# Inverse roots on VectorE for four tiles at once, and layernorm and gate as a queue of small jobs, in a sparse attention and expert kernel

## The chip, the cores and the metric

The kernel runs on one core of a Trainium2 chip. A core has five engines that run their own instruction streams in order and wait for one another by semaphores: TensorE (PE in the profile, its weight loads as PEld), VectorE (DVE), ScalarE (ACT), GpSimd (POOL) and SyncE (SP). The metric is the device time of one execution in microseconds, as the median of several runs.

## The reference

The input is a graph of 4096 nodes with 512 features and a 0/1 adjacency. The layer is an attention over neighbours with 8 heads of 64, then a mixture of 8 experts of which each node takes the best 2. Both read a layernorm and are added to their input.

```python
def _layernorm(x, axis=-1, eps=1e-5):
    m = jnp.mean(x, axis=axis, keepdims=True)
    v = jnp.var(x, axis=axis, keepdims=True)
    return (x - m) / jnp.sqrt(v + eps)

# attention
adj = jnp.maximum(adjacency_matrix, eye)
q, k, v = (jnp.einsum('nd,hdk->hnk', node_matrix, W) for W in (Wqs, Wks, Wvs))
scores = jnp.einsum('hqk,hmk->hqm', q, k) * kd ** (-0.5)
scores = scores + IDENTITY_BIAS * eye - MASK_VAL * (1.0 - adj)
att = jax.nn.softmax(scores, axis=-1)
return jnp.einsum('hqm,hmk,hko->qo', att, v, Wo)

# experts
logits = xf @ Wg + bg
topk_scores, topk_idx = jax.lax.top_k(logits, 2)
topk_w = jax.nn.softmax(topk_scores, axis=-1)
h = jax.nn.gelu(jnp.einsum('nd,edh->neh', xf, W1) + b1, approximate=False)
y = jnp.einsum('neh,ehf->nef', h, W2) + b2
# the sum of topk_w * y over the two chosen experts

x = x + attention(_layernorm(x), adj, ...)
x = x + experts(_layernorm(x), ...)
```

## The kernel before

The kernel goes through three stages. The projection stage takes 32 tiles of 128 nodes through layernorm and the projections to q, k and v, which go to DRAM, and beside this makes for each tile a list of the nodes that are a neighbour of any of its 128 queries. The attention stage goes through 395 items: for each tile its own 128 keys and then, 363 in all, chunks of 128 keys of its list. GpSimd gathers the rows of k and v and of the adjacency of each chunk by indirect DMA, 7 items ahead. The expert stage runs 71 tiles of sorted nodes through the two matrices of their expert.

The layernorm's mean and variance are taken on VectorE; the inverse root (a first guess from the bits of the number and three Newton steps) on GpSimd, for one tile at a time, one number per partition:

```python
def mean_var(pool, xin, name):
    stats = pool.tile([P, nc.vector.BN_STATS_DIM], F32, tag="stats", name=f"stats_{name}")
    nc.vector.bn_stats(stats, xin)
    mv = pool.tile([P, nc.vector.BN_AGGR_DIM + 2], F32, tag="mv", bufs=6, name=f"mv_{name}")
    nc.vector.bn_aggr(mv[:, :2], stats)
    nc.gpsimd.tensor_scalar(mv[:, 1:2], mv[:, 1:2], EPS, None, op0=ALU.add)      # L155
    nc.gpsimd.tensor_scalar(                                                     # L157
        mv[:, 2:3].bitcast(I32), mv[:, 1:2].bitcast(I32), -0.5, float(0x5F3759DF),
        op0=ALU.mult, op1=ALU.add,
    )
    m, v, r, t = (mv[:, j : j + 1] for j in range(4))
    for _ in range(3):
        nc.gpsimd.tensor_scalar(t, r, r, v, op0=ALU.mult, op1=ALU.mult)          # L163
        nc.gpsimd.tensor_scalar(t, t, -0.5, 1.5, op0=ALU.mult, op1=ALU.add)      # L164
        nc.gpsimd.tensor_mul(r, r, t)                                            # L165
    nc.gpsimd.tensor_scalar(t, m, r, -1.0, op0=ALU.mult, op1=ALU.mult)           # L166
    return mv

def normalize(pool, dst, xin, mv, name):
    nc.scalar.activation(dst, xin, AF.Identity, bias=mv[:, 3:4], scale=mv[:, 2:3])   # L171
```

One step of the attention stage fetches an item far ahead, transposes the keys of item n+3, takes the scores of n+2, the values of n, and then does what is due of the tiles that have ended (`later`). `masked` is the product of the exponentials with the mask, and `values` ends with the running sum of the exponentials, both on VectorE.

```python
for n, (i, c) in enumerate(items):
    if n + AHEAD < len(items):
        fetch(n + AHEAD)          # L687: two indirect DMAs by GpSimd; one scatter (L565) if any waits
    # ...
    if n + 3 < len(items):
        turn(n + 3)               # PE L703, ACT L706
    if n + 2 < len(items):
        scores(n + 2)             # PE L719, ACT L729
    values(n)                     # PE L748, DVE L754
    later(n)
    if n + 2 < len(items):
        masked(n + 2)             # DVE L736
    if c == listed[i] - 1:
        left.append((n, i))
```

`later(n)` calls `piece(i, n - n0)` for the tiles that have ended: each piece k is due k steps after the end of its tile. The `e` buffers are two banks of PSUM.

```python
def piece(i, k):
    # ...
    if k == 1:      # sums of the exponentials over the keys, for 8 heads in 4 x 32 rows and 2 halves
        sums[i] = ps_e.tile([P, 2, P], F32, tag="e", name=f"sums_{i}")
        a = acc.pop(i).rearrange("k (r j u) q -> k r u j q", r=2, u=2)
        for r in range(4):
            nc.tensor.matmul(
                sums[i][r * Q4 : (r + 1) * Q4], ones32, a[:, r % 2, r // 2],
                start=True, stop=True, tile_position=(0, r * Q4),
            )
    if k == 2:
        rinv[i] = single.tile([P, 2, P], F32, tag="rinv", name=f"rinv_{i}")
        nc.vector.reciprocal(rinv[i], sums[i])                                   # L776
        # ... a test of the sums on ACT (L778)
        load_x(i)
    if k == 3:      # the reciprocals spread over the rows of each head
        # ... 2 matmuls of 256 columns (L783), and a test of rinv on ACT
    if k == 4:
        o = osb[i]
        nc.vector.tensor_mul(o, o, rb.pop(i).rearrange("p j u q -> p (j u) q"))
    if k == 5:
        # ... 4 matmuls with Wo (L795)
    if k == 6:
        xt = x_in[i]
        nc.vector.tensor_add(xt, xt, py.pop(i))
        nc.sync.dma_start(out=out[ts(i, P), :], in_=xt)
        mv[i] = mean_var(small, xt, f"b{i}")
    if k == 7:
        # ... rows of a group of tiles, once per group
        normalize(small, row[g][:, j, :D], x_in.pop(i), mv.pop(i), f"b{i}")
    if k == 8:
        x2T[i] = gate_1(i, row[g][:, j, :D], single, ps_e, "e")    # 4 transposes (PE L177), copy (ACT L178)
    if k == 9:
        l4[i] = gate_2(i, x2T.pop(i), single, ps_e, "e")           # gate product (PE), copy (ACT)
    if k == 10:
        gate_3(i, l4.pop(i), lg[g][:, j], ps_e, "e")               # logits (PE), bias (DVE)
    if j < m - 1:
        return
    # k == 11 to 14, once per group of m tiles: ranks, places, weights, then scatters of the rows
```

Groups have 4 tiles, and the last three have 2, 1 and 1. Ranks count the nodes that went to each expert before:

```python
    for j in range(m):
        nc.vector.tensor_copy(counts[:, j], count)
        nc.vector.tensor_add(count, count, chosen[:, j])
```

In the projection stage the same layernorm runs a block of 4 tiles ahead, one tile in a step, with the load of x two steps before its statistics.

Of the kernel before, what the change touches and what calls it, by code (L numbers as in the profile page):

```python
# [32 lines left out]
def kernel(  # L33
# [115 lines left out]
    def mean_var(pool, xin, name):  # L149

        stats = pool.tile([P, nc.vector.BN_STATS_DIM], F32, tag="stats", name=f"stats_{name}")
        nc.vector.bn_stats(stats, xin)
        mv = pool.tile([P, nc.vector.BN_AGGR_DIM + 2], F32, tag="mv", bufs=6, name=f"mv_{name}")
        nc.vector.bn_aggr(mv[:, :2], stats)
        nc.gpsimd.tensor_scalar(mv[:, 1:2], mv[:, 1:2], EPS, None, op0=ALU.add)  # L155

        nc.gpsimd.tensor_scalar(  # L157
            mv[:, 2:3].bitcast(I32), mv[:, 1:2].bitcast(I32), -0.5, float(0x5F3759DF),
            op0=ALU.mult, op1=ALU.add,
        )  # L160
        m, v, r, t = (mv[:, j : j + 1] for j in range(4))
        for _ in range(3):
            nc.gpsimd.tensor_scalar(t, r, r, v, op0=ALU.mult, op1=ALU.mult)  # L163
            nc.gpsimd.tensor_scalar(t, t, -0.5, 1.5, op0=ALU.mult, op1=ALU.add)  # L164
            nc.gpsimd.tensor_mul(r, r, t)  # L165
        nc.gpsimd.tensor_scalar(t, m, r, -1.0, op0=ALU.mult, op1=ALU.mult)  # L166
        return mv

    def normalize(pool, dst, xin, mv, name):

        nc.scalar.activation(dst, xin, AF.Identity, bias=mv[:, 3:4], scale=mv[:, 2:3])  # L171
# [14 lines left out]
    with tc.tile_pool(name="adjT", bufs=3) as ap, tc.tile_pool(  # L186
# [181 lines left out]
        def tokens_1(i):  # L368
            mvs[i] = mean_var(work, xts[i], f"a{i}")

        def tokens_2(i):
            xns[i] = work.tile([P, D], F32, tag="xn", name=f"xn_{i}")
            normalize(work, xns[i], xts.pop(i), mvs.pop(i), f"a{i}")
# [67 lines left out]
        for t in range(TPB):  # L441
            tokens_2(t)
            tokens_3(t)
        list_constants()


        load_at = {7 * i // 4: i for i in range(NT)}
        lists_from = {7 * (g * G + G - 1) // 4 + 3: g for g in range(NTB)}
        for u in range(8 * NTB + 1):
            b, s = divmod(u, 8)  # L450
            if u in load_at:
                load_adj(load_at[u])
            due = []
            for k in range(8):
                if u - k in lists_from:
                    due += lists_at(lists_from[u - k], k)
            nxt = (b + 1) * TPB
            if b < NTB:
                if b + 1 < NTB:
                    if s < 4:  # L460
                        load_x(nxt + s)
                    if 2 <= s < 6:
                        tokens_1(nxt + s - 2)
                    if 3 <= s < 7:
                        tokens_2(nxt + s - 3)
                if s < 4:
                    project_kv(b, s)
                else:
                    if s == 4:
                        qT = block.tile([P, NP, TB], F32, tag="qT", name=f"qT_{b}")  # L470
                    project_q(b, s - 4, qT)
                    if s == 7:
                        nc.sync.dma_start(out=qT_d[:, :, ts(b, TB)], in_=qT)
                if b + 1 < NTB and s >= 4:
                    tokens_3(nxt + s - 4)
            if u - 2 in load_at:
                neighbours(load_at[u - 2])
            for f in due:
                f()


    def gate_1(i, row, pool, psum, tag):

        xT = pool.tile([P, DC, P], F32, tag="x2T", name=f"x2T_{i}")
        transposed(psum, xT, row, f"b{i}", tag)
        return xT

    def gate_2(i, xT, pool, psum, tag):
        pg = psum.tile([P, P], F32, tag=tag, name=f"pg_{i}")
        for c in range(DC):  # L490
            nc.tensor.matmul(
                pg[c * Q4 : (c + 1) * Q4], wg[:, c, :], xT[:, c, :], start=True, stop=True,
                tile_position=(0, c * Q4),
            )
        l4 = pool.tile([P, P], F32, tag="l4", name=f"l4_{i}")
        nc.scalar.copy(l4, pg)
        return l4

    def gate_3(i, l4, l, psum, tag):
        pl = psum.tile([P, E], F32, tag=tag, name=f"pl_{i}")  # L500
        nc.tensor.matmul(pl, l4, gather4, start=True, stop=True)
        nc.vector.tensor_add(l, pl, bg_sb)

    def route_1(m, l, pool, name):
# [15 lines left out]
        for j in range(m):  # L520
            nc.vector.tensor_copy(counts[:, j], count)
            nc.vector.tensor_add(count, count, chosen[:, j])
        return rank, chosen, counts

    def route_2(m, chosen, counts, psum, tag, name):

        pp = psum.tile([P, m, E], F32, tag=tag, name=f"pp_{name}")
        nc.tensor.matmul(pp, below, chosen, start=True, stop=False)
        nc.tensor.matmul(pp, ones, counts, start=False, stop=True)
# [108 lines left out]
    with tc.tile_pool(name="kv", bufs=AHEAD + 1) as kvp, tc.tile_pool(  # L638
# [14 lines left out]
        spread = single.tile([P, 2, P], F32, name="spread")  # L653
        nc.vector.memset(spread, 0.0)
        for u in range(2):
            for r in range(2):
                q = (2 * u + r) * Q4
                nc.vector.memset(spread[q : q + 1, u, r * KD : (r + 1) * KD], 1.0)
# [100 lines left out]
        DONE = "e"  # L759

        def piece(i, k):
# [3 lines left out]
            if k == 1:  # L765

                sums[i] = ps_e.tile([P, 2, P], F32, tag="e", name=f"sums_{i}")
                a = acc.pop(i).rearrange("k (r j u) q -> k r u j q", r=2, u=2)
                for r in range(4):
                    nc.tensor.matmul(  # L770
                        sums[i][r * Q4 : (r + 1) * Q4], ones32, a[:, r % 2, r // 2],
                        start=True, stop=True, tile_position=(0, r * Q4),
                    )
            if k == 2:
                rinv[i] = single.tile([P, 2, P], F32, tag="rinv", name=f"rinv_{i}")
                nc.vector.reciprocal(rinv[i], sums[i])  # L776
                test = single.tile([P, 2, P], F32, tag="test", name=f"test_{i}")
                nc.scalar.activation(test, sums.pop(i), AF.Copy, accum_out=fine[:, i, 0:1])  # L778
                load_x(i)
            if k == 3:  # L780
                rb[i] = ps_e.tile([P, 2, 2, P], F32, tag="e", name=f"rb_{i}")
                for u in range(2):
                    nc.tensor.matmul(  # L783
                        rb[i][:, :, u, :], spread[:, u], rinv[i], start=True, stop=True
                    )
                test = single.tile([P, 2, P], F32, tag="test", name=f"test2_{i}")
                nc.scalar.activation(test, rinv.pop(i), AF.Copy, accum_out=fine[:, i, 1:2])
            if k == 4:
                o = osb[i]
                nc.vector.tensor_mul(o, o, rb.pop(i).rearrange("p j u q -> p (j u) q"))  # L790
# [7 lines left out]
            if k == 6:  # L798
                xt = x_in[i]
                nc.vector.tensor_add(xt, xt, py.pop(i))  # L800
                nc.sync.dma_start(out=out[ts(i, P), :], in_=xt)
                mv[i] = mean_var(small, xt, f"b{i}")
            if k == 7:
                if j == 0:
                    row[g] = small.tile([P, m, W], F32, tag="rows", name=f"rows_{g}")
                    lg[g] = small.tile([P, m, E], F32, tag="l", name=f"l_{g}")
                    nc.vector.tensor_copy(
                        row[g][:, :, D].bitcast(I32), ids[:, i0 : i0 + m]
                    )
                normalize(small, row[g][:, j, :D], x_in.pop(i), mv.pop(i), f"b{i}")  # L810
            if k == 8:
                x2T[i] = gate_1(i, row[g][:, j, :D], single, ps_e, "e")
            if k == 9:
                l4[i] = gate_2(i, x2T.pop(i), single, ps_e, "e")
            if k == 10:
                gate_3(i, l4.pop(i), lg[g][:, j], ps_e, "e")
            if j < m - 1:
                return
            if k == 11:
                ranks[g] = route_1(m, lg[g], small, f"{g}")  # L820
            if k == 12:
                rank, chosen, counts = ranks[g]
                ranks[g] = rank, route_2(m, chosen, counts, ps_e, "e", f"{g}")
            if k == 13:
                rank, pp = ranks.pop(g)
                slots_i[g] = route_3(m, lg.pop(g), rank, pp, row[g], small, f"{g}")
            if k == 14:
                for t in range(m):
                    for s in range(2):
                        waiting.append(lambda t=t, s=s: route_4(row[g], slots_i[g], t, s))  # L830

        LAST = 14
        left = []

        def later(n):
            for n0, i in left:
                piece(i, n - n0)

# [9 lines left out]
        for n, (i, c) in enumerate(items):  # L848
            if n + AHEAD < len(items):
                fetch(n + AHEAD)  # L850
# [21 lines left out]
        for n in range(len(items), len(items) + LAST + 1):  # L872
            later(n)
            while waiting:
                waiting.pop(0)()

# [26 lines left out]
    with tc.If(again > 0):  # L903
# [81 lines left out]
        with tc.tile_pool(name="g3", bufs=1) as one, tc.tile_pool(  # L985
# [4 lines left out]
            with tc.For_i(0, N, P) as t0:  # L990
# [5 lines left out]
                m = mean_var(one, xt, "g")  # L996
                normalize(one, rows[:, 0, :D], xt, m, "g")
                xT = gate_1("g", rows[:, 0, :D], one, psum, "a")
                lg4 = gate_2("g", xT, one, psum, "b")
                l = one.tile([P, 1, E], F32, name="gl")  # L1000
                gate_3("g", lg4, l[:, 0], psum, "c")
# [146 lines left out]
```

## Time and profile before

| | |
|---|---|
| median of 3 runs | 2644.12 us (2635.33 to 2649.11) |
| the profiled execution | 2492.47 us, span 2490.7 us |
| PE, PEld busy | 2175.0 us (87%), 1449.5 us (58%) |
| DVE, ACT, POOL busy | 1522.2 us (61%), 968.8 us (39%), 1467.1 us (59%) |
| first gather, last gather | 413 us, 1838 us |
| first matmul of the expert stage | 1926 us |

Busy time is the time in which an engine executes; issuing, waiting and semaphores are not in it. A share of the whole span mixes three stages with different limits, so windows of time and the waits of each stage tell more. In the answers, `out<-in` names the tiles that an instruction writes and reads, and L with a number is a line of the kernel. The profiled execution is shorter than the timed runs; stage lengths below are those of the profiled one.

### The profile page before, as it was taken

How to read it: one execution, taken by the hardware profiler on the slowest of the kernel's cores; microseconds unless marked ns; L12 is line 12 of the kernel's file. 1: busy time of each engine (PE TensorE's matmuls, PEld its weight loads, DVE VectorE, ACT ScalarE, POOL GpSimd, SP SyncE). 2: the span in 40 equal slices, each digit the busy share in tenths (PEclk: the TensorE clock that was granted, in tenths of full speed). 3: DMA queues.
4: the chain of work that ended last, by engine and by line, in shares of the span. 5: the costliest groups of instructions: out<-in, count | busy, mean ns of one | idle time of the engine just before them, and what ended most of it. 6: DMA issues, size and time to landing. Idle time of an engine off the chain costs nothing. (4 is left out here: it accounts for less than half of the span.)

```text
span 2490.7 us, 50730 instructions
## 1 busy us (share of the span) xinstructions
PE 2175.0 (87%) x19898; PEld 1449.5 (58%) x19898; DVE 1522.2 (61%) x2101; ACT 968.8 (39%) x1834; POOL 1467.1 (59%) x1711
## 2 busy tenths in 40 slices
PE   6899997888888997988988888878872999999998
PEld 3344444777776775776766767666651444444444
DVE  3787782877777786777777777767662233333332
ACT  2222221555554553555554545545430222222222
POOL 4665564877877787787888878778751122112111
PEclk9999998989988998998999999989885999999999
DMA  6758873666667676666666566556536656656654
GB/s 266 275 203 309 306 279 139 184 193 212 197 209 222 211 217 213 197 218 195 202 181 200 182 188 211 185 178 188 184 121 218 135 136 137 133 137 139 136 134 96
DMA packets 176341, 477.35 MB, mean 192 GB/s; under 512 B 22705, under 2 KB 43185, under 8 KB 172002
## 3 DMA queue, kind: packets, MB, share of 16 engines
q0 software_dynamic: 79232, 249.68, 34.6%
q1 hardware_dynamic: 91490, 213.87, 26.7%
q10 hardware_dynamic: 5376, 10.49, 1.2%
q8 instruction: 162, 2.65, 0.4%
q14 instruction: 81, 0.66, 0.1%
HBM read 402.23 MB, written 71.72 MB: 190 GB/s over the span
## 5 line engine op out<-in xcount | busy, mean ns | idle before, releaser
L736 DVE TENSOR_TENSOR e<-e,mask 128x1024 f32<-128x1024 f32 x363 | 442.9, 1220 | 257.8 <-ACT e L729 256.8
L687 POOL DMA_INDIRECT kv<-kv_d,key_of x363 | 460.7, 1269 | 144.9 <-issue 65.4
L687 POOL DMA_INDIRECT mask<-in_adjT_dram,mask_of x363 | 426.8, 1176 | 110.6 <-issue 81.1
L754 DVE TENSOR_TENSOR acc<-acc,e 128x1024 f32<-128x1024 f32 x363 | 442.2, 1218 | 0.0
L719 PE MATMUL s<-q,kT 64*128 64x128 f32 x5808 | 440.1, 294 | 0.3 <-ACT acc L729 0.3
L729 ACT ACTIVATE e<-s 128x512 f32<-128x512 f32 x726 | 394.3, 596 | 118.1 <-PE s L719 115.4
L748 PE MATMUL po<-e,kv 128*64 128x128 f32 x5808 | 422.2, 291 | 0.0
L1083 POOL DMA_INDIRECT out_dram<-y,r x71 | 110.0, 1550 | 477.6 <-ACT y L1082 357.0
L719 PEld LDWEIGHTS s<-q,kT 64*128 64x128 f32 x5808 | 390.1, 203 | 0.8 <-ACT acc L729 0.6
L748 PEld LDWEIGHTS po<-e,kv 128*64 128x64 f32 x5808 | 331.8, 144 | 48.0 <-issue 8.1
L706 ACT COPY kT<-pk 128x512 f32<-128x512 f32 x395 | 230.9, 585 | 313.2 <-PE pk L703 298.2
L1047 PE MATMUL ph<-w,xT 128*128 x568 | 258.5, 598 | 1.0 <-ACT xT L178 1.0
L1076 PE MATMUL py<-w,hT 128*128 x568 | 255.6, 593 | 0.9 <-DVE hT L1061 0.9
L703 PE MATMUL pk<-ident,kv 64*128 64x64 f32 x2904 | 177.8, 245 | 49.7 <-DMA kv<-kv_d,key_of 43.7
L703 PEld LDWEIGHTS pk<-ident,kv 64*128 64x128 f32 x2904 | 127.2, 146 | 150.5 <-issue 107.0
L1081 DVE TENSOR_TENSOR y<-py,bb 128x512 f32<-128x512 f32 x71 | 49.1, 692 | 225.6 <-PE py L1076 222.4
L324 POOL TENSOR_SCALAR started<-slots,base 128x1152 bf16<-128x1152 f32 (+11 forms) x32 | 126.6, 3960 | 73.5 <-DVE longer L295 37.6
L1047 PEld LDWEIGHTS ph<-w,xT 128*128 128x128 f32 x568 | 103.3, 192 | 104.7 <-issue 103.0
L1076 PEld LDWEIGHTS py<-w,hT 128*128 128x128 f32 x568 | 102.5, 190 | 104.0 <-issue 102.8
L177 PE MATMUL pt_b<-ident,rows 128*128 128x128 f32 x128 | 32.3, 400 | 140.0 <-ACT rows L171 140.0
L267 DVE TENSOR_REDUCE flags<-adjT 128x32 f32<-128x4096 f32 x32 | 140.5, 4400 | 3.1 <-DMA adjT<-in_adjT_dram 2.9
L1052 DVE TENSOR_TENSOR h<-ph,bb 128x512 f32<-128x512 f32 x71 | 49.1, 692 | 141.1 <-PE ph L1047 141.1
(573 smaller groups left out, 2554.2 us busy)
## 6 DMA issues: line engine op xcount, KB each, us to landing
adjT<-in_adjT_dram SPq DMA_DIRECT2D x32, 2048.0 KB, 9.2
bb<-in_L_ffn_b_dram SPq DMA_DIRECT2D x142, 256.0 KB, 5.0
r<-xs_d SPq DMA_DIRECT2D x71, 258.0 KB, 2.7
kv_d<-kv SPq DMA_DIRECT2D x32, 512.0 KB, 3.7
xt<-in_x_dram SPq DMA_DIRECT2D x32, 256.0 KB, 10.3
qT_d<-qT SPq DMA_DIRECT2D x8, 1024.0 KB, 5.9
q<-qT_d SPq DMA_DIRECT2D x32, 256.0 KB, 6.6
xr<-in_x_dram SPq DMA_DIRECT2D x32, 256.0 KB, 5.2
```

What stands on the lines that cost most here:

```text
L267: nc.vector.tensor_reduce(flags[g][:, j, :], adj_in.pop(i), axis=AX.X, op=ALU.max)
L324: nc.gpsimd.tensor_scalar(started[i], slots[:, :n], base[g][:, j : j + 1], None, op0=ALU.is_ge)
L687: nc.gpsimd.indirect_dma_start(out=to, out_offset=None, in_=src, in_offset=bass.IndirectOffsetOnAxis(ap=of[:, s], axis=0),)
L703: nc.tensor.transpose(pk[:, r, ts(p, KD)], kv[n][half, ts(p, P)], ident[half, half])
L706: nc.scalar.copy(kT[n].rearrange("k p (r j) -> k r p j", r=2), pk[:, :, : NP * KD].rearrange("k r (p j) -> k r p j", p=NP),)
L719: nc.tensor.matmul(s[r][:, p, :], k[rows, p, :], q_in[i][rows, p, :], start=True, stop=True,)
L729: nc.scalar.activation(e[:, r * NP : (r + 1) * NP], s[r], AF.Exp)
L736: nc.vector.tensor_mul(e, e, m.unsqueeze(1).to_broadcast([P, 2 * NP, P]))
L748: nc.tensor.matmul(po[i][r * KD : (r + 1) * KD, p, :], v[:, ts(h, KD)], e[:, r * NP + p, :], start=(c < 0 and p == 0), stop=(c == listed[i ...
L754: nc.vector.tensor_add(acc[i], acc[i], e)
L1047: nc.tensor.matmul(ph, xTs[b][:, c, :], w1[:, bass.ds(es[b], 1), c, :], start=(c == 0), stop=(c == DC - 1),)
L1076: nc.tensor.matmul(py, hTs[b][:, c, :], w2[:, bass.ds(es[b], 1), c, :], start=(c == 0), stop=(c == HC - 1),)
```

## The change

The inverse roots leave GpSimd for VectorE and are taken for all tiles of a group (attention stage) or block (projection stage) in one set of 12 instructions; only the very first tile of the kernel has its own set, so that work can begin. To this end the layernorm of the attention stage begins when the last tile of a group has ended. Normalizing, transposing, the gate and the ranks of a group then go into a queue of small jobs, one of which is taken in a step in which no tile has pieces 1, 3 or 5 (those with matmuls) to do. The part of a job on PE is issued at the end of the step, and the part on ACT or DVE at the head of the next. The row of x after attention is written to its place in the group, stored from there, and later normalized in place. The sums are put in 128 rows of 128 columns instead of twice that, so that the reciprocal has half the elements per row. The count within a group is added by matmuls. In the projection stage x is loaded a block earlier, the layernorm has 4 steps for statistics and 4 for the rest, and the adjacency is loaded every 13/8 steps instead of every 7/4.

```diff
-    def mean_var(pool, xin, name):
+    def mean_var(pool, mv, xin, name):
         nc.vector.bn_stats(stats, xin)
         nc.vector.bn_aggr(mv[:, :2], stats)
-        nc.gpsimd.tensor_scalar(mv[:, 1:2], mv[:, 1:2], EPS, None, op0=ALU.add)
-        nc.gpsimd.tensor_scalar(... 0x5F3759DF ...)
+    def inverse_root(mv):
+        m, v, r, t = (mv[:, :, j] for j in range(4))
+        nc.vector.tensor_scalar_add(v, v, EPS)
+        nc.vector.tensor_scalar(
+            r.bitcast(I32), v.bitcast(I32), -0.5, float(0x5F3759DF), op0=ALU.mult, op1=ALU.add
         )
         for _ in range(3):
-            nc.gpsimd.tensor_scalar(t, r, r, v, op0=ALU.mult, op1=ALU.mult)
-            nc.gpsimd.tensor_scalar(t, t, -0.5, 1.5, op0=ALU.mult, op1=ALU.add)
-            nc.gpsimd.tensor_mul(r, r, t)
-        nc.gpsimd.tensor_scalar(t, m, r, -1.0, op0=ALU.mult, op1=ALU.mult)
+            nc.vector.scalar_tensor_tensor(t, r, -0.5, r, op0=ALU.mult, op1=ALU.mult)
+            nc.vector.tensor_mul(t, t, v)
+            nc.vector.scalar_tensor_tensor(r, t, 1.5, r, op0=ALU.add, op1=ALU.mult)
+        nc.vector.scalar_tensor_tensor(t, m, -1.0, r, op0=ALU.mult, op1=ALU.mult)
# ... projection stage
-        load_at = {7 * i // 4: i for i in range(NT)}
+        load_at = {13 * i // 8: i for i in range(NT)}
-                    if s < 4:
-                        load_x(nxt + s)
-                    if 2 <= s < 6:
-                        tokens_1(nxt + s - 2)
-                    if 3 <= s < 7:
-                        tokens_2(nxt + s - 3)
+                    if s < 4:
+                        tokens_1(nxt + s)          # with the root of the block at its last tile
+                    else:
+                        tokens_2(nxt + s - 4)
+                        if b + 2 < NTB:
+                            load_x(nxt + TPB + s - 4)
# ... counts
-        for j in range(m):
-            nc.vector.tensor_copy(counts[:, j], count)
-            nc.vector.tensor_add(count, count, chosen[:, j])
+        nc.vector.tensor_copy(counts, count.unsqueeze(1).to_broadcast([P, m, E]))
+        # one reduce of chosen over the tiles and one add to count; then, on PE, into the places:
+        for j in range(m - 1):
+            nc.tensor.matmul(pp[:, j + 1 :], ones, chosen[:, j]..., start=False, stop=False)
# ... piece 1 and 2
-                sums[i] = ps_e.tile([P, 2, P], F32, tag="e", name=f"sums_{i}")
+                sums[i] = ps_e.tile([P, P], F32, tag="e", name=f"sums_{i}")
+                for t in range(2):
+                    for q in range(4):     # 8 matmuls of 128 columns; half_q has ones in half its columns
-                rinv[i] = single.tile([P, 2, P], F32, tag="rinv", name=f"rinv_{i}")
+                rinv[i] = single.tile([P, P], F32, tag="rinv", name=f"rinv_{i}")
# ... piece 3: 4 matmuls of 128 columns for 2 of 256
# ... piece 6, and the jobs in place of pieces 7 to 14
+                y = row[g][:, j, :D] if m > 1 else x_in[i]
+                nc.vector.tensor_add(y, x_in[i], py.pop(i))
+                nc.sync.dma_start(out=out[ts(i, P), :], in_=y)
+                mean_var(small, mv[g][:, j], y, f"b{i}")
+                if j == m - 1:
+                    jobs.extend(route(g))
+        # route(g): start (root, then normalize tile 0); per tile turn_x, product, logits
+        # (the last also normalizes the next tile); rank; place
         def later(n):
+            busy = False
             for n0, i in left:
                 piece(i, n - n0)
+                busy = busy or n - n0 in (1, 3, 5)
+            if jobs and not busy:
+                then = jobs.pop(0)()
+                if then:
+                    first_of_step.append(then)      # issued at the head of the next step
```

## The prediction

> **What bounds the kernel now.** I read first the windows of the three stages (granted clock and share of each engine), then the waits, then GpSimd's groups inside the attention stage, and last the timeline of one tile's end. The attention stage runs from GpSimd's first gather at 413 us to its last at 1838; its window shows (PE, PEld, DVE, ACT, POOL busy and counts, PE clock, DMA share, GB/s):
>
> ```profile
> 413.00:1838.00 1425.00, 1215.66 (x16636) 981.47 (x16638) 1034.68 (x1171) 724.76 (x1419) 1112.78 (x1141) 0.91 0.64 199
> ```
>
> No engine looks full here. But the waits name one thing on both ACT and PE (waiter, whom it waited for, total us, times, longest):
>
> ```profile
> ACT rows L171 <- POOL mv_b L166: 194.3, 32, 13.3
> ...
> PE pt_b L177 <- ACT rows L171: 140.0, 31, 11.0
> ...
> PE pk L703 <- DMA kv<-kv_d,key_of: 43.7, 21, 3.9
> ```
>
> Layernorm's inverse root of a tile runs on GpSimd; ACT, in order, sits 6.1 us per tile until it ends, and PE 4.4 us until ACT has normalized. The groups of GpSimd from 412 to 1840 (busy us, mean ns | idle before) say more:
>
> ```profile
> L687 POOL DMA_INDIRECT kv<-kv_d,key_of x363 | 460.7, 1269 | 144.9 <-issue 65.4 <-PE po L748 39.1 <-PE pk L703 7.6
> L687 POOL DMA_INDIRECT mask<-in_adjT_dram,mask_of x363 | 426.8, 1176 | 110.6 <-issue 81.1 <-DVE acc L754 16.1 <-DMA kv<-kv_d,key_of 3.7
> L565 POOL DMA_INDIRECT xs_d<-rows,slot_i x56 | 67.3, 1202 | 18.1 <-issue 12.5 <-ACT e L729 2.5 <-DMA xs_d<-rows,slot_i 1.2
> L163 POOL TENSOR_SCALAR mv_b<-mv_b 128x1 f32<-128x1 f32 x90 | 66.5, 739 | 9.7
> L164 POOL TENSOR_SCALAR mv_b<-mv_b 128x1 f32<-128x1 f32 x90 | 25.5, 283 | 7.4
> L157 POOL TENSOR_SCALAR mv_b<-mv_b 128x1 int32<-128x1 int32 x30 | 23.3, 777 | 2.5
> L165 POOL TENSOR_TENSOR mv_b<-mv_b 128x1 f32<-128x1 f32 x90 | 22.5, 250 | 7.5
> L155 POOL TENSOR_SCALAR mv_b<-mv_b 128x1 f32<-128x1 f32 x30 | 13.3, 444 | 9.2 <-DVE mv_b L154 7.7
> L166 POOL TENSOR_SCALAR mv_b<-mv_b 128x1 f32<-128x1 f32 x30 | 7.8, 259 | 3.2
> ```
>
> Add both columns: gathers 460.7+144.9+426.8+110.6 = 1143, scatters 67.3+18.1 = 85, inverse roots 158.9+39.5 = 198. That is 1427 of a window of 1428: nearly all "idle" is a fixed 0.3 us ahead of each gather (a wait on a buffer accounts for only some 23 us of L748's 39.1: 39.1 less 53 x 0.3). GpSimd, 78% busy by its counter, has no room left. **It is the bound of the attention stage**, and 198 us of its queue is arithmetic on one number per row. The end of one tile:
>
> ```profile
> 1034.30 2.46 POOL L163 TENSOR_SCALAR mv_b<-mv_b 128x1 f32<-128x1 f32 x1
> ...
> 1036.82 1.11 PE L719 MATMUL s<-q,kT 64*128 64x128 f32 x16
> ...
> 1041.52 0.81 ACT L171 ACTIVATE rows<-xr,mv_b 128x512 f32<-128x512 f32 x1 [4.84 <-POOL mv_b L166]
> ...
> 1042.39 0.88 PE L177 MATMUL pt_b<-ident,rows 128*128 128x128 f32 x4 [3.44 <-ACT rows L171]
> ...
> 1043.68 2.02 PE L719 MATMUL s<-q,kT 64*128 64x128 f32 x16
> ```
>
> GpSimd issues no gather from 1033.1 to 1041.9; ACT waits 4.84 us, PE 3.44, and the next 16 score matmuls take 2.02 us where they took 1.11.
>
> **What the Trainium skill says.** "SBUF — State Buffer", section "Who interferes with whom": a DVE instruction with two SBUF inputs contends with a GpSimd instruction that reads SBUF. The trace fits: a gather takes 0.94 us at least and up to 2.0 beside DVE's 1.22 us products. So the mean of 1.22 us holds some (1.222-0.943) x 726 = 203 us of contention, and removing GpSimd's arithmetic doesn't remove that. "TensorE: Matmul & The Clock Gate", Part 1, puts the clock at half after an idle window of about 3.4 us; the 1.11 to 2.02 us above, after a gap of 3.44, agrees. "GPSIMD Engine Reference", section 4.1, gives elementwise work to VectorE. "VectorE: DVE Perf Modes" counts some 150 cycles of start per instruction; small DVE operations here take 0.14 to 0.24 us, whether 1, 2 or 4 columns wide, which is why four tiles at once cost as one.
>
> **The change part by part.**
> *Inverse root, attention stage.* Removed from GpSimd: 198 us. Added to DVE: 12 instructions for each of 10 groups; from the rows of the trace 0.17 us for a two-scalar or product form and 0.23 for scalar_tensor_tensor (L1070: 229 ns) give 7 x 0.23 + 5 x 0.17 = 2.5 us, 25 us in all. DVE has 1034.7 busy of 1425, so this fits.
> *Job queue.* Layernorm of a group begins when all of its tiles are there, one small PE job in a step, its ACT or DVE half at the head of the next step. ACT finds its input ready, so the 194 us on ACT and the 133 us of them on PE inside this stage go, and with them the half clock after each gap. They are not added to the 198: both are the same time seen from two engines.
> *Reciprocal.* 1750 ns for 256 columns, about 0.15 of it fixed, so some 0.95 for 128: 0.8 x 32 = 26 us less DVE, and ACT's 48 us wait on it (L778 for L776) about halves. Sums and spreading keep their matmul columns (4x256 becomes 8x128, 2x256 becomes 4x128): PE stays at 0.64 and 1.06 us per tile.
> *Counts.* For a group of four, 8 small DVE operations of 0.17 to 0.21 become 3: 1 us x 7; PE gets 3 tiny matmuls per group. Nothing visible.
> *Projection stage.* At the start xn of the four tiles come 3.9 us apart, the length of one root on GpSimd, and the first projection begins at 24.6 us; with one root for tile 0 and one for three tiles they should be ready near 17, and the weights then decide: 5 us. Later PE waits 11.0 us for xn (15 to 412 us); most goes. Projection itself keeps PE at 371.5 of 397 us. Together 15 us. Adjacency comes sooner (13/8 for 7/4), but gathers must still wait for the projection's end.
> *After attention.* The expert stage does not change. The last groups of 2, 1 and 1 tiles still take 14 steps after the last item; the root shortens by about 2 us, jobs queue behind each other for as much: 0.
>
> *The sum.* GpSimd in the attention stage: 1143+85 = 1228 remain. A shorter stage makes DVE's two-input products (885 us) denser, 62% to 70% of the time; contention grows by 203 x (70/62-1) = 26. Coupling, where PE is briefly behind, less the buffer waits that vanish: 4, a guess. PE's own need is below this: 395 items x 2.36 us (the spacing when nothing is late) = 932, per tile 0.64+1.06+3.7+about 1.1 = 6.5, x 32 = 208, together 1140. So 1425 becomes about 1258, a gain of 167, with the projection stage 182. The profiled execution would be 2491-182 = 2309. The timed runs are 6% longer than the profiled one, and no view says where: subtracting gives 2462, scaling 2644 x 2309/2491 = 2451. I take 2455.
>
> **Rivals.**
> *PE is the bound after all.* If gathers were ahead, only the waits of PE count: 133 us plus the half clock after them; its limit would be 1140 us, and the total could fall to some 2360. Against it: the wait for kv (43.7 us), and a clock of 0.91, which speak of a PE that is fed late.
> *Contention takes the gain.* DVE now has the root too, and gathers stretch towards 1.4 us each: 726 x 0.18 = 130 us lost, leaving 50 us: 2590. For it: up to 2.46 us for a GpSimd operation that takes 0.34 alone. Against it: DVE waits for ACT 257 us now, so there is slack, and DVE's total falls slightly.
> *The transfers are the bound.* DMA share 0.64 would become 0.72 and landing of a gather, 3.7 us at the median, may grow. With 7 items fetched ahead, some 20 us, this should stay hidden; if not, 2520.
> *A new wait.* Normalizing in place must follow the store of that row; jobs hold one of two PSUM buffers for longer; ACT or PE in order could stop there. A step of slack lies between each pair, so I give it 10 to 30 us at most: 2480.
>
> **Range and chances.** Between the PE limit (2360, all but perfect) and contention (2590) I put eight tenths on 2400 to 2535. The removed 198 us sits on a queue that is demonstrably full, so faster by over 2% (under 2591) is 0.95, within 2% 0.04, slower 0.01.
>
> **What would show it.** In the profile after: GpSimd without mv_b, gathers and scatters filling the window of about 1258 us, gather means of 1.22 to 1.28 us; no wait of ACT for mv over 20 us in total; PE clock above 0.95 in the stage; DVE root about 2.5 us per group; reciprocal near 0.95 us; the first projection near 18 us. I am wrong if GpSimd shows idle time for buffers (then PE bounds), if the gathers' mean passes 1.4 us, or if the stage stays above 1350 us.

## The result and the profile after

| | before | after | ratio |
|---|---|---|---|
| median, side by side | 2646.6 us (2635.3 to 2658.3) | 2507.7 us (2497.1 to 2518.9) | 0.9475 [0.9414, 0.9536] |
| the same kernels on the chip of e1 to e4 | 2494 us | 2350.5 us (2346.2 to 2353.1) | 0.9423 [0.9401, 0.9445] |

The change made the kernel faster by 139 us. The forecast was 2455 us, a gain of 189; the measured time lies in its range. The sets of runs fell on several chips: e1 to e4 on one, e5 to e8 on a second that is as fast (before takes 2494 us on both), e9 to e12 on a third (2671 us). Which chips the first runs had is not known; the timed ones (2646 us) are near the third, the first profile of before (span 2490.7 us) is near the first two. So "the quicker chip" stands below for the first two and "the slower chip" for the others, and times are compared within a set, or across sets as ratios to the kernel before. What follows is the profile of after from a quicker chip (span 2348.7 us); the slower one has a part of its own below.

The attention stage now runs from GpSimd's first gather at 412.8 us to its last at 1702.1, 1289 us where it was 1425. The projection stage ends at 413 as before, and from the last gather to the end it is 647 us for 653. So all of the gain but 6 us lies in the attention stage. Its window (length, then busy PE, PEld, DVE, ACT, POOL with counts, PE clock, DMA share, GB/s):

```profile
413.00:1704.00 1291.00, 1169.88 (x17015) 960.14 (x17017) 1024.94 (x1217) 722.66 (x1419) 964.66 (x777) 0.95 0.69 219
```

All of GpSimd's groups in it (busy us, mean ns | idle ahead of it, and what ended most of that):

```profile
L724 POOL DMA_INDIRECT kv<-kv_d,key_of x363 | 465.7, 1283 | 174.5 <-PE po L785 85.4 <-issue 45.5 <-PE pk L740 16.2
L724 POOL DMA_INDIRECT mask<-in_adjT_dram,mask_of x362 | 430.4, 1189 | 114.0 <-issue 92.7 <-DMA kv<-kv_d,key_of 5.5 <-DVE acc L791 4.8
L592 POOL DMA_INDIRECT xs_d<-rows,slot_i x52 | 68.8, 1323 | 38.7 <-ACT e L766 21.7 <-issue 9.4 <-ACT acc L766 4.8
```

The inverse root's rows are gone. Busy and idle added row by row give 640.2 + 544.4 + 107.5 = 1292 us, the window. GpSimd's queue is still the length of the stage, but now part of it is real waiting: "PE po L785", the values matmul that frees a key buffer, ended 85.4 us of idle time, and scatters stood 38.7 us for 18.1 before. The waits of the same stage (waiter, whom it waited for, total us, times, longest):

```profile
POOL kv L724 <- PE po L785: 85.4, 79, 7.4
PE pk L740 <- DMA kv<-kv_d,key_of: 81.5, 52, 6.4
...
ACT less L580 <- DVE less L579: 29.4, 7, 5.4
...
ACT rows L171 <- DVE mv L167: 15.3, 8, 2.9
```

In this stage ACT's wait for the layernorm fell from 175 us (194 in the whole kernel) to 15. In its place stand a circle, PE waiting for gathered keys (81.5 us, from 43.7) while GpSimd waits for PE to give buffers back, and, once per group, a wait that has grown from 15 us to 29: ACT for "less", the difference of two logits, which VectorE makes in the step in which ACT is to take its exponential.

### The profile page after: what moved, and what is told of

Its sections match the earlier page's. It is cut to its first block, busy times and chain, and to the rows that moved or that the text cites. A ratio compares the mean times of both kernels' runs of the same rounds, so it can differ in the third digit from the quotient of the medians.

```text
span 2509.9 us, 51012 instructions
## 1 busy us (share of the span) xinstructions
PE 2245.3 (89%) x20304; PEld 1496.0 (60%) x20304; DVE 1533.4 (61%) x2300; ACT 963.5 (38%) x1834; POOL 1233.7 (49%) x943
## 5 line engine op out<-in xcount | busy, mean ns | idle before, releaser
L724 POOL DMA_INDIRECT kv<-kv_d,key_of x363 | 479.7, 1322 | 324.3 <-PE po L785 191.5
L756 PE MATMUL s<-q,kT 64*128 64x128 f32 x5808 | 481.0, 295 | 34.2 <-issue 23.6
L724 POOL DMA_INDIRECT mask<-in_adjT_dram,mask_of x363 | 435.7, 1200 | 116.4 <-issue 100.6
L785 PE MATMUL po<-e,kv 128*64 128x128 f32 x5808 | 438.1, 292 | 11.7 <-issue 10.8
L756 PEld LDWEIGHTS s<-q,kT 64*128 64x128 f32 x5808 | 414.7, 201 | 51.5 <-issue 33.1
L785 PEld LDWEIGHTS po<-e,kv 128*64 128x64 f32 x5808 | 335.9, 144 | 69.8 <-issue 28.0
L740 PE MATMUL pk<-ident,kv 64*128 64x64 f32 x2904 | 186.7, 243 | 70.7 <-DMA kv<-kv_d,key_of 31.6
L178 ACT COPY xT<-pt_e 128x512 f32<-128x512 f32 x71 | 41.6, 586 | 240.0 <-PE pt_e L177 237.1
```

Of the source, the lines that this page charges most:

```text
L724: nc.gpsimd.indirect_dma_start(out=to, out_offset=None, in_=src, in_offset=bass.IndirectOffsetOnAxis(ap=of[:, s], axis=0),)
L740: nc.tensor.transpose(pk[:, r, ts(p, KD)], kv[n][half, ts(p, P)], ident[half, half])
L756: nc.tensor.matmul(s[r][:, p, :], k[rows, p, :], q_in[i][rows, p, :], start=True, stop=True,)
L785: nc.tensor.matmul(po[i][r * KD : (r + 1) * KD, p, :], v[:, ts(h, KD)], e[:, r * NP + p, :], start=(c < 0 and p == 0), stop=(c == listed[i ...
```

## The experiments

**e1, the kernel before again.** No edit.

> The kernel before, unchanged, for a second trace of it: its first trace lasted 2491 us where its timed runs lasted 2635 to 2658, and the changed kernel's trace of 2510 us has an attention stage that is no shorter (gathers 412 to 1864) than that of 413 to 1838. If the first trace was an unusually short execution, this one lasts about 2640 us and its attention stage about 1570 us, with waits that the first one lacks. If profiling shortens this kernel, it lasts about 2490 us again.

2501.4 us, gathers from 412.9 to 1844.3 us. The first profile was an ordinary one of a quicker chip. The "6%" between timed and profiled runs that the prediction could not place is thus most likely the difference between two chips.

**e2, the kernel after, on the same chip as e1.** No edit.

> The changed kernel, unchanged, beside the parts: 2500 us (ratio to before 0.947) and a trace of the same length, with GpSimd waiting some 190 us for buffers that PE has not freed.

2350.5 us, ratio 0.9423 (the times expected for e2, e3 and e4 are those of the slower chip). The expected 190 us of GpSimd waiting for buffers were 62: 85.4 less 79 times the fixed 0.3 us.

**e3, the whole change with the root left on GpSimd.**

```diff
                 mean_var(small, mv[g][:, j], y, f"b{i}")
+                pool_root(mv[g][:, j])      # the 12 GpSimd instructions of before, per tile
...
             def start():
-                inverse_root(mv[g])
                 return lambda: norm(0)
```

> The changed kernel, but in the attention stage the inverse root of each tile is taken on GpSimd again, in the same 12 instructions of one column, at once after the tile's statistics; normalizing still comes later from the job queue, so ACT does not wait for it. Full GpSimd (my theory): its queue gets back 198 us, of which contention hides nothing, so most of the gain of the attention stage is lost: 2600 to 2640 us. Waits of ACT and PE for the root (the rival): the waits stay away, so 2500 to 2530 us.

2546.7 us, ratio 1.0207 [1.0182, 1.0232]: some 2% slower than before, where 2600 to 2640 us on the slower chip meant a ratio of 0.98 to 1.00. Neither ACT nor PE waits for the root here (the queue gives it many steps of slack), and yet the whole gain is lost. GpSimd's groups in its attention stage, in the columns of the fence above:

```profile
L738 POOL DMA_INDIRECT mask<-in_adjT_dram,mask_of x362 | 433.3, 1197 | 114.3 <-issue 92.6 <-DVE acc L805 8.2 <-DMA kv<-kv_d,key_of 5.8
L738 POOL DMA_INDIRECT kv<-kv_d,key_of x363 | 427.3, 1177 | 122.4 <-issue 60.5 <-PE po L799 25.0 <-PE s L770 13.7
L164 POOL TENSOR_SCALAR mv<-mv 128x1 f32<-128x1 f32 x90 | 123.0, 1367 | 9.7
L606 POOL DMA_INDIRECT xs_d<-rows,slot_i x53 | 66.5, 1254 | 16.2 <-issue 11.9 <-ACT e L780 2.1 <-ACT kT L757 1.5
L166 POOL TENSOR_TENSOR mv<-mv 128x1 f32<-128x1 f32 x90 | 48.3, 537 | 7.5
L165 POOL TENSOR_SCALAR mv<-mv 128x1 f32<-128x1 f32 x90 | 45.4, 504 | 7.4
L158 POOL TENSOR_SCALAR mv<-mv 128x1 int32<-128x1 int32 x30 | 22.4, 747 | 2.5
L167 POOL TENSOR_SCALAR mv<-mv 128x1 f32<-128x1 f32 x30 | 14.8, 494 | 3.2
L157 POOL TENSOR_SCALAR mv<-mv 128x1 f32<-128x1 f32 x30 | 11.9, 396 | 16.2 <-DVE mv L153 14.8
```

The roots take 265.8 + 46.5 = 312 us of the queue where they took 198 in the kernel before, most likely because ACT no longer stands still and VectorE's products go on beside them: the first product of a Newton step has a mean of 1367 ns for 739, and 340 ns at least. With gathers 1097 and scatters 83 this is 1492 us, the stage (1489). As long as GpSimd's queue is full, the wait of ACT that the queue of jobs removes is worth nothing by itself; what counts is the time on GpSimd.

**e4, the kernel before with the root on VectorE, and nothing else.**

```diff
-            nc.gpsimd.tensor_scalar(t, r, r, v, op0=ALU.mult, op1=ALU.mult)
-            nc.gpsimd.tensor_scalar(t, t, -0.5, 1.5, op0=ALU.mult, op1=ALU.add)
-            nc.gpsimd.tensor_mul(r, r, t)
+            nc.vector.scalar_tensor_tensor(t, r, -0.5, r, op0=ALU.mult, op1=ALU.mult)
+            nc.vector.tensor_mul(t, t, v)
+            nc.vector.scalar_tensor_tensor(r, t, 1.5, r, op0=ALU.add, op1=ALU.mult)
# and so for the other instructions of the root; still per tile, no queue
```

> The kernel before, with one thing changed: the 12 instructions of the inverse root of each tile run on VectorE, still one tile at a time and with ACT waiting for them in its old place. Full GpSimd: 198 us leave its queue, so most of the gain comes, 2500 to 2540 us. Waits: a wait of 6.1 us per tile becomes some 3 to 4, so about a third to a half of the gain, 2570 to 2610 us.

2365.3 us, ratio 0.9489 [0.9469, 0.9509], so 129 us of the 144 come from this edit alone. ACT was expected to wait 3 to 4 us per tile still, but in the attention stage ACT waits for the root no more, and PE no more for the rows. So e4 alone does not tell a full GpSimd from the waits; e3 does. Its attention stage is even shorter than that of after, 1275 us. But its gathers start at 440 us: the projection stage is 27 us longer. From 15 to 412 us VectorE is busy 333 us there for 275 before, and PE 354 for 372. GpSimd's groups of the attention stage:

```profile
L685 POOL DMA_INDIRECT kv<-kv_d,key_of x363 | 468.9, 1292 | 144.7 <-issue 56.4 <-PE po L746 42.8 <-PE s L717 12.5
L685 POOL DMA_INDIRECT mask<-in_adjT_dram,mask_of x363 | 462.7, 1275 | 111.4 <-issue 83.2 <-DMA kv<-kv_d,key_of 6.1 <-DVE mv_b L163 4.9
L563 POOL DMA_INDIRECT xs_d<-rows,slot_i x56 | 72.6, 1296 | 18.0 <-issue 12.5 <-ACT e L727 2.5 <-ACT test L785 1.2
```

Against after, the wait for PE's values matmul is half (42.8) and the scatters wait 18.0 us, as before the change; but the gathers are longer, 1292 and 1275 ns for 1283 and 1189.

**e5, gathers ten ahead.** `AHEAD = 7` becomes `AHEAD = 10` in the kernel after: ten items fetched ahead into eleven buffers.

> The changed kernel with gathers 10 items ahead for 7, in 11 buffers for 8. If the missing gain is coupling (GpSimd waits 62 us beyond its fixed 0.3 us for a buffer that PE has not freed, and PE 82 us for a gather), both waits shrink: 2305 to 2335 us on this chip, where the changed kernel takes 2350. If GpSimd's queue is simply full, nothing changes: 2345 to 2355.

2313.8 us (2297.2 to 2327.7), ratio 0.9264 [0.922, 0.9309]. As the theory of coupling had it: the wait for PE falls to 39.3 us in 80 times, of which 24 are the fixed 0.3, and the stage to 1240 us:

```profile
L724 POOL DMA_INDIRECT mask<-in_adjT_dram,mask_of x362 | 450.1, 1243 | 110.3 <-issue 79.2 <-DMA kv<-kv_d,key_of 9.4 <-DVE acc L791 7.9
L724 POOL DMA_INDIRECT kv<-kv_d,key_of x363 | 449.9, 1239 | 132.1 <-issue 45.1 <-PE po L785 39.3 <-PE s L756 15.2
```

Some of the 49 us of the stage is lost again behind it: from the last gather to the first matmul of the expert stage 99 us pass for 81.

**e6, after with the projection stage of before** (its per-tile root on GpSimd, its order of steps, 7/4 in place of 13/8).

> The changed kernel with the projection stage of before: roots on GpSimd one tile at a time, x loaded as before, adjacency every 7/4 steps. By my sum the new projection stage is worth 15 us: 2365. By the two traces, in which the first gather starts at 413 us both times, it is worth nothing: 2345 to 2355.

2356.8 us, ratio 0.9456 [0.9423, 0.949]: the new projection stage is worth some 6 us, within the intervals nothing. It is needed all the same, as e4 shows: a root per tile on VectorE costs 27 us there without it.

**e7, after without the queue**: the new projection stage, the root on VectorE per tile, and the fixed steps 7 to 14 and the sums of 256 columns of before.

> The projection stage of the changed kernel, and the attention stage of before with one thing changed: the root of each tile by 12 instructions on VectorE, no job queue, sums in twice 128 columns. If the queue takes waits away, as it is meant to, this is slower than the changed kernel: 2360 to 2375. If the queue costs something, as the two attention stages of 1291 us with it and 1277 without suggest, it is faster: 2330 to 2340.

2335.6 us (2330.2 to 2342.3), ratio 0.9367 [0.9337, 0.9397]. **Without the queue of jobs the kernel is 15 us faster** than after on the chip of e2, and 18 us faster than e8 below, which has the queue and was timed beside it. GpSimd's wait for the values matmul is 48.7 us (85.4 in after), the scatters' idle time 17.1 (38.7), ACT's wait for "less" 14.1 (29.4):

```profile
L706 POOL DMA_INDIRECT kv<-kv_d,key_of x363 | 470.7, 1297 | 152.7 <-issue 53.4 <-PE po L767 48.7 <-PE pk L722 15.8
L706 POOL DMA_INDIRECT mask<-in_adjT_dram,mask_of x363 | 460.0, 1267 | 111.4 <-issue 83.5 <-DVE acc L773 4.6 <-DVE mv_b L166 4.6
L584 POOL DMA_INDIRECT xs_d<-rows,slot_i x56 | 74.6, 1332 | 17.1 <-issue 11.6 <-ACT e L748 1.9 <-DMA kv<-kv_d,key_of 1.2
```

The idle time of these three groups is 281 us, for 327 in after, but the stage is only 6 us shorter: here too the gathers are longer than in after.

**e8, after with the sums of 256 columns.**

> The changed kernel with sums, reciprocal and spreading of before (reciprocal of 128x256). It gives 26 us back to VectorE and lengthens ACT's wait for the reciprocal. Off the path, as VectorE and ACT are not the bound: 2345 to 2356. If ACT's wait counts: about 2370.

2353.4 us, ratio 0.9442 [0.9411, 0.9473]: the reciprocal of half the width is worth 3 us, not to be told from none.

**What the queue costs.** The timeline of after, where the last job of a group puts its second half at the head of a step (start, length, engine; in brackets the idle time before and what ended it):

```profile
772.79 0.15 DVE L579 TENSOR_TENSOR less<-top 128x4 f32<-128x4 f32 x1
772.98 0.20 ACT L580 ACTIVATE less<-less 128x4 f32<-128x4 f32 x1 [4.38 <-DVE less L579]
773.09 0.57 ACT L743 COPY kT<-pk 128x512 f32<-128x512 f32 x1
...
773.71 0.46 PE L740 MATMUL pk<-ident,kv 64*128 64x64 f32 x8 [2.62 <-ACT kT L743]
...
774.01 1.64 PE L756 MATMUL s<-q,kT 64*128 64x128 f32 x16
...
775.01 1.08 POOL L592 DMA_INDIRECT xs_d<-rows,slot_i  x1 [2.56 <-ACT e L766]
```

ACT stands 4.38 us before an exponential of four columns; the copy of keys behind it is late, PE stands 2.62 us for the copy, and its next 16 score matmuls take 1.64 us for 1.11. GpSimd, which was given the scatter at once, stands 2.56 us. Two edits, both on the slower chip (the times expected are again those of a quicker one), take these waits away:

**e12, the scatters one job later.**

```diff
                 def then():
                     slots_i[g] = route_3(m, lg.pop(g), r, pp, row[g], small, f"{g}")
-                    for t in range(m):
-                        for s in range(2):
-                            waiting.append(lambda t=t, s=s: route_4(row[g], slots_i[g], t, s))
                 return then
+            def release():                       # a job of its own, after place
+                for t in range(m):
+                    for s in range(2):
+                        waiting.append(lambda t=t, s=s: route_4(row[g], slots_i[g], t, s))
```

> The kernel after, with the scatters alone handed to GpSimd one job later; the exponential stays at the head of the step, behind VectorE. No work is left out. If GpSimd's wait before the scatters is what costs: 2335 to 2343 us, as the run with both. If ScalarE's exponential is what costs: 2346 to 2354 us, while the run with both falls. If neither: both at 2346 to 2354 us.

**e9, the same, and the exponential a step later too**: a job "weights" between place and release issues ACT's exponential at the end of a step, and VectorE's rest of the routing at the head of the next.

> The kernel after, with the last job of a group (place) cut in three: the exponential of the two logits' difference one step after VectorE made its operand, VectorE's rest of the routing at the head of the step after, and the group's scatters handed to GpSimd only once all of it is issued, one job later. No work is left out. Theory 1 (the queue's 15 us over per-tile jobs are the waits at the end of a group: GpSimd, which takes its instructions in order, stands before a scatter whose operands VectorE and ScalarE make in that very step, and ScalarE's exponential stands before VectorE, ahead of the copies of keys): 2333 to 2343 us, GpSimd's idle time before the scatters from 39 us down to 17 to 22, ScalarE's wait for less from 29 to 37 us down to below 12. Theory 2 (the 15 us are elsewhere in the queue: the norm behind the group's root, the halves of a job at the head of a step before VectorE's product): 2346 to 2354 us, as the kernel after, though those two waits shrink.

e12 takes 2514.7 us (2510.8 to 2516.7), ratio 0.941 [0.9388, 0.9432]; e9 2497.9 us (2490.1 to 2506.7), ratio 0.9355 [0.9321, 0.939]. In e12 the scatters' idle time falls to 17.7 us (from 36.8 in after on a chip of this speed) and nothing is gained beyond the interval of after; in e9 ACT's wait for "less" falls from e12's 18.4 us to 3.9, and the same chip is 17 us faster. So what costs is the exponential at the head of the step, together with VectorE's rest of the routing, which e9 moves as well, and e9 has by ratio what e7 has without any queue. The reservation is that this chip is bound differently (next part), and that after was not timed in this set; on the quicker chip the two edits were not tried. A later release also costs at the end: from the last gather to the first expert matmul 89.5 us in e9 and 95.8 in e12, 83.9 in after.

**e10, e7 with gathers ten ahead, and e11, e9 with gathers ten ahead**, on the slower chip as well.

> The kernel with per-tile roots on VectorE, the jobs of each tile at fixed steps, the new projection stage and sums of 256 columns (e7), and gathers ten ahead in place of seven. No work is left out. If the two gains add (15 us without the queue, 37 us from three more buffers): 2295 to 2305 us, attention stage about 1240 us. If three more buffers already hide what the queue costs: 2310 to 2320 us, as the kernel after with ten ahead.

> The kernel after with the later scatters and exponential, and gathers ten ahead. No work is left out. If the waits at the end of a group and the waits for buffers are separate losses: 2297 to 2307 us. If ten ahead hides the former already: 2310 to 2320 us. If PE is by then the bound (it was busy 1161 of 1262 us with ten ahead): no attention stage below 1230 us, so not below 2290 us.

2484.7 us, ratio 0.9311 [0.9289, 0.9333], and 2489.5 us, ratio 0.9308 [0.9277, 0.934]. Ten ahead, worth 37 us in e5, is worth 8 here (e11 for e9), within the scatter of the runs, and both ratios lie above those expected (0.920 to 0.930). By ratio e5, e7, e9, e10 and e11 beat both kernels; e5 has the best one, but on a quicker chip, so that it cannot be ranked against e10 and e11.

**What the slower chip shows.** In the trace of after that belongs to the timed runs the projection stage ends at 412.4 us and the end takes 646, as on the quicker chip; all 161 us lie in the attention stage, 1452 us. Its window and two of GpSimd's groups:

```profile
413.00:1864.00 1451.00, 1286.70 (x16979) 1026.31 (x16979) 1022.20 (x1215) 716.02 (x1412) 974.91 (x777) 0.92 0.63 195
```

```profile
L724 POOL DMA_INDIRECT kv<-kv_d,key_of x363 | 479.7, 1322 | 324.3 <-PE po L785 191.5 <-PE pk L740 48.0 <-issue 45.7
L724 POOL DMA_INDIRECT mask<-in_adjT_dram,mask_of x362 | 433.7, 1198 | 116.1 <-issue 100.3 <-DVE acc L791 5.8 <-DVE e L773 4.3
```

The gathers take as long as on the other chip (1322 and 1198 ns for 1283 and 1189), DVE and ACT have the same busy time, but PE is busy 1287 us for 1170 at a clock of 0.92 for 0.95, and GpSimd waits 191.5 us for its values matmul. The single matmul is hardly slower (the score matmuls have a median of 272 ns in both traces, a mean of 295 for 287). What this trace has more of is time in which PE stands before an instruction that waits for nothing the profile shows ("issue"), also in the middle of a set of matmuls:

```profile
PE pk L740 <- issue: 34.8, 47, 14.1
...
PE s L756 <- issue: 22.5, 51, 1.6
...
PE po L785 <- issue: 16.0, 35, 1.4
```

All such waits of PE in this stage add up to 85 us, for a single one of 14.5 us on the quicker chip. So here GpSimd's queue is not full and waits for PE, and three more buffers hide little; but PE is busy 89% of the stage, no more than the 91% on the quicker chip, so it comes late without being fuller. What holds PE's instructions up, and where the kernel before loses its 150 to 180 us there, stays open; no trace of before was taken on this chip.

## Why the prediction was right, and where it was not

**GpSimd is the bound, and its 198 us are the gain: right.** This is shown for the quicker chip. e3 keeps the root on GpSimd and removes every wait of ACT and PE for it: slower than before. e4 moves the root and leaves the rest of the program as it was: 90% of the gain. Reading ACT's 194 us and PE's 133 us as the same time, not to be added, was right.

On the slower chip, where the timed runs fell, it is not shown. In their own trace two of the signs occur by which the prediction was to be wrong: GpSimd is idle for buffers (191.5 us for PE's values matmul), and the stage is 1452 us, above 1350. The sum was worked out for a trace of one chip and scaled to times of another, so it owes something to luck that 2508 us lies in the range. What the sum itself was worth is seen on the quicker chip, where 144 us came for 182.

**The sum: 1425 became 1289, not 1258.** Term by term, from the first profile of before and that of e2:

| term | predicted | measured | from |
|---|---|---|---|
| roots off GpSimd's queue | -198 | -198 | the rows are gone |
| contention, gathers and scatters longer | +26 | +10 | busy 954.8 to 964.9 us |
| coupling less buffer waits | +4 | +54 | idle 273.6 to 327.2 us |
| projection stage | -15 | 0 (e6: -6) | first gather at 413 in both |
| end | 0 | -6 | 653 to 647 us |
| sum | -183 (-182 in the prediction, by rounding) | -140 | spans: 2490.7 - 2348.7 = 142 |

**The step that failed is "Coupling, where PE is briefly behind, less the buffer waits that vanish: 4, a guess".** It measured 54: 30 ahead of the keys' gathers, 21 ahead of the scatters, 3 ahead of the masks'. That these are waits for buffers which PE frees late is what e5 tests: with three more buffers the idle time ahead of the gathers is below that of before, and 37 us come back. But a shorter queue does not bring such waits by itself, as the kernels without the queue of jobs show (from the rows above; means and idle time of both gathers, and busy and idle time of the scatters added up):

| kernel | gathers, mean ns | busy us | idle ahead of them | scatters | stage |
|---|---|---|---|---|---|
| before | 1222 | 887.5 | 255.5 | 85.4 | 1425, of it 198 for the roots |
| after | 1236 | 896.1 | 288.5 | 107.5 | 1289 |
| e5, after with ten ahead | 1241 | 900.0 | 242.4 | 103.3 (48 of them, 52 to 56 in the others) | 1240 |
| e4, no queue | 1283 | 931.6 | 256.1 | 90.6 | 1275 |
| e7, no queue | 1282 | 930.7 | 264.1 | 91.7 | 1283 |

In e4 and e7 the coupling is the few us that the sum allowed. It is the queue of jobs, or what comes with it, that makes PE late, though the prediction had credited it with a step of slack between each pair; that slack is missing in the one place where VectorE's second half of "place" and ACT's exponential share the head of a step. The rival "a new wait" (10 to 30 us at most) was thus right in size, if not in the places that it named: the queue costs 15 us in all. It costs no more because without it the gathers are 46 ns longer, some 35 us. VectorE is busier there (1084 us in e7 for 1025), with a root per tile and the wider reciprocal. So the root for four tiles at once may be what keeps the gathers short in after and e5; no run has it without the queue, so this is not shown.

**Contention, 26 predicted, 10 measured** (with five instructions fewer in the window, which are worth some 6 us). In e4 and e7 it is some 50. The rival that it takes the gain is refuted all the same: no mean of a gather passes 1300 ns on the quicker chip, and the rival had 1400. That it exists shows in e3, where the roots grew by 114 us. VectorE can be the one that suffers: the Trainium skill, "SBUF — State Buffer", section "Who interferes with whom", lists tensor_scalar among the forms that can take the ports which VectorE shares with GpSimd, and says that whoever issues first then blocks the other for the whole instruction. The trace of after agrees, beside GpSimd's building of lists in the projection stage:

```profile
99.62 5.43 POOL L324 TENSOR_SCALAR started<-slots,base 128x2048 bf16<-128x2048 f32 x1 [2.33 <-PE pr L337]
...
100.21 4.86 DVE L158 TENSOR_SCALAR mv<-mv 128x4 f32<-128x4 f32 x1
...
107.33 0.81 ACT L171 ACTIVATE xn<-xt,mv 128x512 f32<-128x512 f32 x1 [8.73 <-DVE mv L167]
...
108.20 1.12 PE L177 MATMUL pt_a<-ident,xn 128*128 128x128 f32 x4 [5.22 <-ACT xn L171]
```

The root's first instruction, 0.17 us elsewhere, ends with GpSimd's: 4.7 us of the 8.73 that ACT stands before it normalizes, and PE stands 5.22 behind it.

**The projection stage: its first half right, its sum wrong.** The first projection matmul starts at 20.15 us for 24.55 (near 18 was predicted), so the 5 us came. They are gone by 413 us. PE's wait for xn fell only from 11.0 to 8.0 us, not "most", and 5.22 of the rest is the wait just shown. What else holds this stage at 413 us was not traced further.

**Transfers** were hidden, as said: DMA share 0.69, and the wait for keys belongs to the circle with PE that e5 widens. **PE is the bound** was wrong on the quicker chip. On the slower one GpSimd does wait for PE, so this rival's refutation ("a PE that is fed late") held for the trace that was read and not for every chip.

**Small steps.** The root took 12 instructions of 0.17 us, a few longer, 2.1 us per group for 2.5 predicted: scalar_tensor_tensor was taken at 0.23 us from a row of another shape and took 0.17. The reciprocal was 0.95 predicted and is 0.95:

```profile
L817 DVE RECIPROCAL rinv<-sums 128x128 f32<-128x128 f32 x31 | 29.5, 950 | 0.0
```

Its 26 us on VectorE were worth 3 at most (e8), as VectorE was never the bound. The stage's clock was to exceed 0.95 and is 0.95.

## What to carry to other kernels

Find the engine whose instructions plus their fixed gaps add up to the stage, even if its busy share reads 78%, and take work off that engine; the eye-catching wait of another engine for it may be worth nothing by itself. When that queue is shortened, look next at two losses that trade against each other: the buffers that come back late from the engine that frees them, and the longer instructions of an engine that no longer waits. Here three more buffers removed the first and kept most of the second away (e5). And a queue of jobs must not put a producer and its consumer at the head of the same step: an in-order engine stands there, with all that is queued behind it.

## What was not expected of the hardware

- A small GpSimd instruction can lengthen more than a gather beside VectorE's products: 128 x 1 products went from 739 to 1367 ns on average when VectorE no longer stood still beside them, while the gathers' means went from 1269 and 1176 ns to 1177 and 1197 (e3).
- A one-input VectorE instruction on 4 columns took 4.86 us beside one GpSimd instruction of 5.43 us.
- Chips differ by 6% to 7% on the same kernel (2494 us on two of them, 2671 on a third, 2646 in the first timed runs). For after, all of the difference is in the attention stage, with a PE clock of 0.92 for 0.95 and 85 us for 14.5 in which PE stands at instructions that wait for nothing visible. It changes what an edit is worth: ten ahead gave 37 us on a quicker chip and 8 on the slower.
